# All edges but the fillers gathered by indirect DMA on one queue: the single-row loads of two other queues removed

## The chip, the cores and the metric

The kernel runs on one core of one Trainium2 chip. The metric is the device time in microseconds. The text calls the engines PE (TensorE), DVE (VectorE), ACT (ScalarE), POOL (GpSimd) and SP (SyncE).

## The reference

A graph layer over N = 50000 nodes with 128 features and E = 1650000 edges, sorted by target node. The edges hold one self edge per node. Each edge takes its source node's row through one of two weight matrices (by its type), the messages are summed per target, the node's own transform is added, then come ReLU, the residual and a norm without gain or offset.

```python
def _L0_gnn_ref(X, edge_index, edge_types, W_data, b_data, W_control, b_control, W_self, b_self):
    src, dst = (edge_index[0], edge_index[1])
    Xs = X[src]
    m_data = Xs @ W_data.T + b_data
    m_ctrl = Xs @ W_control.T + b_control
    msg = jnp.where((edge_types == 0)[:, None], m_data, m_ctrl)
    agg = jax.ops.segment_sum(msg, dst, num_segments=X.shape[0])
    out = agg + (X @ W_self.T + b_self)
    return jax.nn.relu(out)
...
x = _layernorm(x + _L0_gnn_ref(x, edge_index, edge_type_2, ...), axis=-1)
```

## The kernel before

The sum over edges is made before the weights: for each target node the source rows are summed per edge type, and only those sums are multiplied by the two weight matrices.

The sorted edge list is cut into 435 blocks. A middle block has 3800 edges: four steps (Q = 4) of seven chunks of 128 edges (R = 7, CH = 128) with 22 fillers each (F = 22), and at its end 128 edges (X) taken as single rows. The first and the last block are "plain": they have only chunks. For each chunk POOL issues one indirect DMA (L451) that gathers 128 rows of x, 64 KB, into a tile `y`. The pool of these tiles has 70 buffers, so that POOL can run ahead of its consumer. PE multiplies `y` by a one-hot matrix `oh` (L454) and adds up a step's seven chunks in a PSUM tile `acc`. The columns of `oh` are W target nodes, counted from the step's first target, for each of two edge types, so a step may not reach over more than W nodes. Two small matmuls (L457) add edge counts for the bias.

The fillers are edges that stand in the places of self edges: a self edge's source row is already in the block's window of x, so its chunk slot is given to a filler's source index, and the sum is put right with matrices made by `fill` and the `left_out_...` functions. `fill(b)` makes the index list `idxs[b]` that the gathers read, five blocks ahead (RAHEAD).

The 128 single rows of a block are loaded in `single_rows` (L434 and L439): SP and ACT each read 64 row offsets into registers and issue 64 DMAs of 512 bytes into a tile `yx`, a quarter of them in each step, two blocks ahead (AHEAD). The offsets come from a DVE op (`offsets`, L425). `yx` is a 29th chunk at the end of the block's last step (C1 = C + 1).

The instructions stand in program order on each engine (a manual schedule, written out in one loop over blocks). A block's four `add`s on DVE (L465) put `acc` into `sums`, a ring of three. Between blocks, ACT copies the overlapping part of the sums to the next ring entry (`take_over`, L470). On ACT's queue that copy stands behind the row DMAs of the block before. DVE then adds the left-out self edges (L363), PE makes the layer of the finished block (L475 to L478), DVE and ACT its norm (L483 to L497), and SP stores it (L498). SP also loads the windows of x (L387, L389) and, every ten blocks, the edge lists.

At the end the flag `bad` is computed. It is above 0 if a step reached over more than W nodes or had fewer than F self edges; then `general`, a slower program for any edge list, runs as well and overwrites the result.

Of the kernel before, what the change touches and what calls it, by code (L numbers as in the profile page):

```python
# [13 lines left out]
I32 = mybir.dt.int32  # L14
U8 = mybir.dt.uint8
AF = mybir.ActivationFunctionType
# [6 lines left out]
N = 50000  # L23
D = 128
ROW = 4 * D
E = 1650000
# [7 lines left out]
R = 7  # L34
W = 38
Q = 4
B = 128
C = R * Q
X = 128
C1 = C + 1  # L40
F = 22
BE = C * CH + Q * F + X
NBLK = 2 + (E - C * CH) // BE
# [5 lines left out]
GROUPS = -(-NBLK // GB)  # L49
GC = GB * C1  # L50
AHEAD = 2
# [27 lines left out]

def straight(ctx, tc, c, x, x_t, src_t, dst_t, etype_t, src_f, dst_f, etype_f, src_x, dst_first, first_p, out):  # L80


# [66 lines left out]

    one_g = {}  # L150

    def load_edges(g):
        t = eds.tile([1, GB * X], I32, name="one_g")
        nc.sync.dma_start(t, src_x[None, g * GB * X:(g + 1) * GB * X])
        one_g[g] = t
        loads[g] = {}
        for name, a in (("s", src_t), ("d", dst_t), ("t", etype_t)):
            t = eds.tile([P, GB, C1], I32, name=name, bufs=1)
            nc.sync.dma_start(t.rearrange("p b c -> p (b c)"), a[:, g * GC:(g + 1) * GC])
            loads[g][name] = t  # L160
        for name, a in (("sf", src_f), ("df", dst_f), ("tf", etype_f)):
            t = eds.tile([GS, F], I32, name=name, bufs=1)
            nc.sync.dma_start(t, a[g * GS:(g + 1) * GS, :])
            loads[g][name] = t
# [69 lines left out]
    def columns(g):  # L234

        a = loads.pop(g)
        first = begin[:, g * GB:(g + 1) * GB, :]
        steps = "p b (q r) -> p b q r"

        def first_of(rel, d):  # L240
            yield (rel[:, :, :C].rearrange(steps, r=R), d[:, :, :C].rearrange(steps, r=R),
                   first[:, :, :, None].to_broadcast([P, GB, Q, R]))
            yield rel[:, :, C:], d[:, :, C:], first[:, :, Q - 1:]

        def first_of_f(rel, d):
            yield rel, d, begin_p[:, g:g + 1].to_broadcast([GS, F])

        h = eds.tile([P, GB, Q, R + 1], BF16, name="h_loop", bufs=1)  # L250
        nc.vector.memset(h, 0.0)
        nc.vector.tensor_tensor(h[:, :, :, :R], a["s"][:, :, :C].rearrange(steps, r=R),
                                a["d"][:, :, :C].rearrange(steps, r=R), op=ALU.is_equal)
        rank = ps_r.tile([P, GB * Q, R + 1], F32, name="rank")
        hs_ = h.rearrange("p b q r -> p (b q) r")
        nc.tensor.matmul(rank, below, hs_, start=True, stop=False)
        for r in range(R):
            nc.tensor.matmul(rank[:, :, r + 1:], ones_b, hs_[:, :, r:r + 1].to_broadcast([P, GB * Q, R - r]),
                             start=False, stop=r == R - 1)

        col, rel = columns_of(a["d"], a["t"], first_of, "")
        check(a["d"], rel, [stats[:, 0, m, g:g + 1] for m in range(2)], "")
        col_f, rel_f = columns_of(a["df"], a["tf"], first_of_f, "_f")
        check(a["df"], rel_f, [stats[:GS, 1, m, g:g + 1] for m in range(2)], "_f")
        v = packed(a["s"], col, "")
        v_f = packed(a["sf"], col_f, "_f")

        cb = eds.tile([P, GB, C], F32, name="cb")
        nc.vector.tensor_scalar(cb, a["t"][:, :, :C], 0.0, float(P), op0=ALU.not_equal, op1=ALU.mult)
        nc.vector.tensor_tensor(cb, cb, a["d"][:, :, :C], op=ALU.add)  # L270
        nc.vector.tensor_tensor(cb, cb, base[:, g * GB:(g + 1) * GB, :].to_broadcast([P, GB, C]), op=ALU.subtract)


        rk = eds.tile([P, GB, C], F32, name="rk")
        nc.vector.scalar_tensor_tensor(rk.rearrange(steps, r=R), h[:, :, :, :R], -LOOP,
                                       rank.rearrange("p (b q) r -> p b q r", q=Q)[:, :, :, :R],
                                       op0=ALU.mult, op1=ALU.add)
        at = Q if g == 0 else 0
        n = (min((g + 1) * GB, NBLK - 1) - g * GB) * Q
        nc.vector.tensor_reduce(loops[:, g:g + 1], rank[:, at:n, R:], AX.XY, ALU.min)  # L280
        stay = eds.tile([P, GB, C], F32, name="stay")
        nc.vector.scalar_tensor_tensor(stay, rk, F - LOOP, v[:, :, :C], op0=ALU.is_ge, op1=ALU.mult)
        col_g[g], rk_g[g], stay_g[g], cb_g[g], vp_g[g] = col, rk, stay, cb, v_f
        if g == GROUPS - 1:
            idxs[NBLK - 1] = a["s"][:, NBLK - 1 - g * GB, :]
# [11 lines left out]
    def fill(b):  # L297
# [20 lines left out]
        nc.vector.tensor_single_scalar(idx, vi, 7, op=ALU.logical_shift_right)  # L318
        nc.vector.scalar_tensor_tensor(col_g[g][:, i, :C], idx, -float(P), vi, op0=ALU.mult, op1=ALU.add)
        idxs[b] = idx  # L320
# [44 lines left out]
    def chunks_of(b, q):  # L365

        n = C1 if not plain(b) else C if b == 0 else RCH if b < NBLK else 0
        return range(q * R, max(q * R, min((q + 1) * R if q < Q - 1 else C1, n)))

# [6 lines left out]
    bys, pcs, zs, pls = {}, {}, {}, {}  # L376
    ats = {}
    ohs, cnts, ys, accs, xws, xTs, pos, hs, mvs, sds = {}, {}, {}, {}, {}, {}, {}, {}, {}, {}

# [12 lines left out]
    def onehot(b):  # L392
        g, i = divmod(b, GB)
        n = C1 if not plain(b) else C if b == 0 else RCH
        oh = ohp.tile([P, C1, 2 * W], F32, name="oh")
        nc.vector.tensor_tensor(oh[:, :n, :], col_g[g][:, i, :n, None].to_broadcast([P, n, 2 * W]),  # L396
# [3 lines left out]
    def counts(b):  # L400

        cnt = ohp.tile([P, Q, 2 * W], BF16, name="cnt")
        with nc.allow_low_precision(reason="whole numbers up to R + 1"):
            whole = [q for q in range(Q) if len(chunks_of(b, q)) == R]
# [9 lines left out]

    SHARE = X // 2
    TURN = SHARE // Q
    RANGE = dict(min_val=0, max_val=(N - 1) * ROW, skip_runtime_bounds_check_because="where a node's row is")
    x_bytes = x.rearrange("n d -> (n d)").bitcast(U8)[None, :]

    def offsets(b):  # L420

        if not plain(b):
            g, i = divmod(b, GB)
            ats[b] = stp.tile([1, X], I32, name="at_x", bufs=AHEAD + 2)
            nc.vector.tensor_scalar(ats[b], one_g[g][:, i * X:(i + 1) * X], float(ROW), None, op0=ALU.mult)  # L425

    def single_rows(b, q):

        if q == 0:
            ys[b] = stp.tile([X, D], F32, name="yx", bufs=AHEAD + 2)  # L430
        both = []
        for j, (eng, dma) in enumerate(((SP, nc.sync), (ACT, nc.scalar))):
            at = j * SHARE + q * TURN
            _, rows = nc.values_load_multi_w_load_instructions(  # L434
                ats[b][0:1, at:at + TURN], engines=[eng], **RANGE)
            both.append([(dma, at + k, row) for k, row in enumerate(rows)])
        for pair in zip(*both):
            for dma, k, row in pair:
                dma.dma_start(ys[b][k:k + 1, :].bitcast(U8), x_bytes[:, bass.ds(row, ROW)])  # L439

    def products(b, q):
# [3 lines left out]
        for k in ks:  # L445
            if k == C:
                r, y = X, ys.pop(b)
            else:
                r = LAST if b == NBLK - 1 and k == RCH - 1 else P
                y = gat.tile([P, D], F32, name="y")  # L450
                nc.gpsimd.indirect_dma_start(  # L451
                    out=y[:r], out_offset=None, in_=x,
                    in_offset=bass.IndirectOffsetOnAxis(ap=idxs[b][:r, k:k + 1], axis=0))
            nc.tensor.matmul(acc[:, :2, :].rearrange("p t w -> p (t w)"), y[:r], ohs[b][:r, k, :],  # L454
                             start=k == ks[0], stop=k == ks[-1])
# [43 lines left out]

    for b in range(1, AHEAD + 1):  # L500
        offsets(b)
    columns(0)
# [6 lines left out]
    for b in range(1, RAHEAD):  # L509
# [3 lines left out]
        if b < AHEAD:  # L513
            onehot(b)
            counts(b)
            for q in range(Q):
                single_rows(b, q)
        if b == 1:
            clear_sums()
    for b in range(NBLK + 1):  # L520
# [16 lines left out]
        for q in range(Q):  # L537
# [24 lines left out]
            if q == 3:  # L562
                left_out_matrix(b + RAHEAD)
                offsets(b + AHEAD + 1)
            if not plain(b + AHEAD):
                single_rows(b + AHEAD, q)

# [251 lines left out]
def gnn_resnorm(  # L819
# [9 lines left out]
    etype_f: bass.AP,  # L829
    src_x: bass.AP,  # L830
    dst_first: bass.AP,
# [38 lines left out]
    with ExitStack() as own:  # L870
        straight(own, tc, c, x, x_t, src_t, dst_t, etype_t, src_f, dst_f, etype_f, src_x,
                 dst_first, first_p, out)
# [56 lines left out]
```

## Time and profile before

| | |
|---|---|
| Median of 10 runs | 15296.68 us (15284.49 to 15308.16) |
| The profiled execution | 15307.44 us |
| Its span on the page | 15305.4 us |
| POOL busy | 11521.9 us (75%) |
| PE busy | 7782.3 us (51%) |
| DVE busy | 6916.8 us (45%) |
| ACT busy | 353.7 us (2%) |
| Share of the 16 DMA engines, q0 (indirect) | 20.0% |
| Share of the 16 DMA engines, q1 and q10 | 3.4% and 0.4% |
| Mean granted TensorE clock | 1.000 |

Register, branch, semaphore and DMA-issuing instructions of a queue are not counted as busy, so ACT and SP can be occupied with issuing DMAs and still show almost no busy time. A group's row gives the instruction count, busy time and mean of one in ns, then the engine's idle time before these instructions and what ended most of it. A line of waits gives total us, times and the longest in us.

### The profile page before, as it was taken

To read this page: it belongs to the slowest core of one execution; us is meant where nothing else is said; L and a number is where in the kernel's file an instruction comes from. 1 tells how busy PE (TensorE), PEld (TensorE's weight loads), DVE (VectorE), ACT (ScalarE), POOL (GpSimd) and SP (SyncE) were. 2 spreads that over 40 slices of the span, in tenths; PEclk is the share of its full clock that TensorE was granted. 3 is DMA by queue.
4 is the path that set the end of the run, shared out by engine and by line. 5 is a ranking of instruction groups with operands and counts; after the bars stand their busy time and mean duration, and the time that the engine had idled before them with its cause. 6 is when DMAs were issued, how large, how long until landed. Compare 5 with 4: busy or idle time off the path is not lost.

```text
span 15305.4 us, 239078 instructions
## 1 busy us (share of the span) xinstructions
PE 7782.3 (51%) x34233; PEld 6914.0 (45%) x34234; DVE 6916.8 (45%) x12861; ACT 353.7 (2%) x875; POOL 11521.9 (75%) x12170
## 2 busy tenths in 40 slices
PE   4444444455555555666665544444444444444444
PEld 3444444444444444444444444444444444444444
DVE  5444444444444444444444444444444444444443
ACT  0000000000000000000000000000000000000000
POOL 7777777777777777777777777777777777777776
DMA  2222222222222222222222222222222222222222
GB/s 66 63 64 63 63 63 65 63 64 63 63 63 64 63 63 63 65 63 63 63 63 63 63 65 63 63 63 63 65 63 63 63 63 63 63 64 63 63 63 53
DMA packets 724494, 968.72 MB, mean 63 GB/s; under 512 B 282787, under 2 KB 522534, under 8 KB 722897
## 3 DMA queue, kind: packets, MB, share of 16 engines
q0 software_dynamic: 389120, 797.69, 20.0%
q1 hardware_dynamic: 277914, 141.12, 3.4%
q10 hardware_dynamic: 55862, 14.50, 0.4%
q14 instruction: 1315, 10.76, 0.2%
q8 instruction: 283, 4.64, 0.1%
HBM read 923.55 MB, written 28.66 MB: 62 GB/s over the span
## 4 chain that ended last, share of the span: by engine, by line
DMA 44%; ACTq 18%; issue 13%; SPq 11%; PE 8%; DVE 5%; ACT 1%; POOL 1%; DVEq 0%; POOLq 0%
DMA yx<-in_x 33%; ACTq L439 14%; SPq L439 9%; PE acc L454 6%; DMA y<-in_x,idx 6%; ACTq L434 3%; DMA out<-o 2%; DMA xT<-in_x_t 2%; DVE sums L363 1%; ACT sums L470 1%; POOL y L451 1%; DMA xw<-in_x 1%; SPq L381 1%; ACTq L468 1%; DMA vf_all<-vd 1%
## 5 line engine op out<-in xcount | busy, mean ns | idle before, releaser
L451 POOL DMA_INDIRECT y<-in_x,idx x12152 | 11512.8, 947 | 3711.9 <-issue 2069.0
L454 PE MATMUL acc<-oh,y 128*128 128x76 f32 x24320 | 6242.0, 429 | 1407.5 <-DMA y<-in_x,idx 1387.1
L454 PEld LDWEIGHTS acc<-oh,y 128*128 128x128 f32 x24320 | 5552.3, 327 | 1945.8 <-DMA y<-in_x,idx 1846.3
L363 DVE TENSOR_TENSOR sums<-pl,sums 128x384 f32<-128x384 f32 x433 | 241.6, 558 | 7506.5 <-ACT sums L470 7506.5
L349 PE MATMUL pl<-z,ones_b 88*128 88x256 bf16 x433 | 170.1, 393 | 3636.5 <-DVE sums L363 3553.3
L349 PEld LDWEIGHTS <-ones_b 88*128 88x128 bf16 x433 | 45.5, 105 | 3681.6 <-DVE sums L363 3681.6
L406 DVE TENSOR_REDUCE cnt<-oh 128x228 bf16<-128x1596 f32 (+2 forms) x435 | 1277.1, 2936 | 0.1
L333 PE MATMUL small<-ones_b,by 128*88 128x1 bf16 x433 | 99.0, 229 | 2246.6 <-DVE by L326 2153.7
L333 PEld LDWEIGHTS <-by 128*88 128x88 bf16 x433 | 64.2, 148 | 2289.5 <-DVE by L326 2289.1
L396 DVE TENSOR_TENSOR oh<-col,small 128x2204 f32<-128x2204 f32 (+2 forms) x435 | 1049.9, 2414 | 0.0
L457 PEld LDWEIGHTS <-to_row 128*128 128x128 bf16 x3476 | 633.5, 194 | 0.0
L465 DVE TENSOR_TENSOR sums<-acc,sums 128x114 f32 x1738 | 475.0, 273 | 298.4 <-PE acc L457 213.9
L326 DVE TENSOR_REDUCE by<-old 128x88 bf16<-128x616 f32 x433 | 577.9, 1335 | 14.8
L470 ACT COPY sums<-sums 128x384 f32 x434 | 222.2, 512 | 14154.5 <-DMA yx<-in_x 13437.5
L478 PE MATMUL po<-wmsgT,sums 128*128 128x128 f32 x1740 | 531.5, 461 | 0.0
L411 DVE TENSOR_REDUCE cnt<-oh 128x76 bf16<-128x608 f32 x434 | 503.9, 1161 | 0.0
L457 PE MATMUL acc<-cnt,to_row 128*128 128x38 bf16 x3476 | 473.5, 220 | 0.0
L478 PEld LDWEIGHTS po<-wmsgT,sums 128*128 128x128 f32 x1740 | 403.3, 322 | 97.5 <-issue 97.5
L307 DVE TENSOR_TENSOR m<-rk,small 128x616 f32<-128x616 f32 x433 | 344.5, 796 | 14.7
L310 DVE TENSOR_TENSOR new<-m,small 128x616 f32<-128x616 f32 x433 | 344.4, 795 | 14.8
L314 DVE TENSOR_REDUCE v_new<-new 128x28 f32<-128x616 f32 x433 | 344.2, 795 | 14.8
L476 PE MATMUL po<-bias,sums 3*128 3x128 f32 x870 | 344.5, 497 | 1.2 <-DVE sums L465 1.2
(116 smaller groups left out, 4064.8 us busy)
## 6 DMA issues: line engine op xcount, KB each, us to landing
yx<-in_x ACTq DMA_DIRECT2D x27712, 0.5 KB
yx<-in_x SPq DMA_DIRECT2D x27712, 0.5 KB
y<-in_x,idx POOLq DMA_INDIRECT x12152
xw<-in_x SPq DMA_DIRECT2D x435, 64.0 KB
xT<-in_x_t SPq DMA_DIRECT2D x435, 64.0 KB
out<-o SPq DMA_DIRECT2D x435, 64.0 KB
vf_all<-vd SPq DMA_DIRECT2D x44, 440.0 KB
s<-in_src_t SPq DMA_DIRECT2D x44, 145.0 KB
```

What stands on the lines that cost most here:

```text
L326: nc.vector.tensor_reduce(by, old.rearrange("p (q r) f -> p q f r", r=R), AX.X, ALU.add)
L363: nc.vector.tensor_tensor(part, pls.pop(b)[:, :, :B], part, op=ALU.add)
L396: nc.vector.tensor_tensor(oh[:, :n, :], col_g[g][:, i, :n, None].to_broadcast([P, n, 2 * W]), num_ps[:, None, :].to_broadcast([P, n, 2 * W ...
L406: nc.vector.tensor_reduce(cnt[:, :n, :], ohs[b][:, :n * R, :].rearrange("p (q r) w -> p q w r", r=R), AX.X, ALU.add)
L411: nc.vector.tensor_reduce(cnt[:, q, :], ohs[b][:, k[0]:k[-1] + 1, :].rearrange("p r w -> p w r"), AX.X, ALU.add)
L434: _, rows = nc.values_load_multi_w_load_instructions(ats[b][0:1, at:at + TURN], engines=[eng], **RANGE)
L439: dma.dma_start(ys[b][k:k + 1, :].bitcast(U8), x_bytes[:, bass.ds(row, ROW)])
L451: nc.gpsimd.indirect_dma_start(out=y[:r], out_offset=None, in_=x, in_offset=bass.IndirectOffsetOnAxis(ap=idxs[b][:r, k:k + 1], axis=0))
L454: nc.tensor.matmul(acc[:, :2, :].rearrange("p t w -> p (t w)"), y[:r], ohs[b][:r, k, :], start=k == ks[0], stop=k == ks[-1])
L457: nc.tensor.matmul(acc[:, 2, :], to_row[:, t, :], cnts[b][:, q, t * W:(t + 1) * W], start=t == 0, stop=t == 1)
L465: nc.vector.tensor_tensor(part, accs.pop((b, q)), part, op=ALU.add)
L478: nc.tensor.matmul(po, a[:, t, :B], c["wmsgT"][:, t * D:(t + 1) * D], start=False, stop=t == 1)
```

## The change

The single rows are taken out. A middle block now has 3672 edges, all in chunks but the fillers, so that there are 450 blocks and not 435; the last one has 11 chunks and not 8. The 29th chunk, `offsets`, `single_rows`, their tiles and their input array go. The one-hot's width W is 36 and not 38.

```diff
-W = 38
+W = 36
 Q = 4
 B = 128
 C = R * Q
-X = 128
-C1 = C + 1
 F = 22
-BE = C * CH + Q * F + X
+BE = C * CH + Q * F
...
-        n = C1 if not plain(b) else C if b == 0 else RCH if b < NBLK else 0
-        return range(q * R, max(q * R, min((q + 1) * R if q < Q - 1 else C1, n)))
+        n = RCH if b == NBLK - 1 else C if b < NBLK else 0
+        return range(q * R, max(q * R, min((q + 1) * R, n)))
...
-    def offsets(b):
-
-        if not plain(b):
-            g, i = divmod(b, GB)
-            ats[b] = stp.tile([1, X], I32, name="at_x", bufs=AHEAD + 2)
-            nc.vector.tensor_scalar(ats[b], one_g[g][:, i * X:(i + 1) * X], float(ROW), None, op0=ALU.mult)
-
-    def single_rows(b, q):
-
-        if q == 0:
-            ys[b] = stp.tile([X, D], F32, name="yx", bufs=AHEAD + 2)
-        both = []
-        for j, (eng, dma) in enumerate(((SP, nc.sync), (ACT, nc.scalar))):
-            at = j * SHARE + q * TURN
-            _, rows = nc.values_load_multi_w_load_instructions(
-                ats[b][0:1, at:at + TURN], engines=[eng], **RANGE)
-            both.append([(dma, at + k, row) for k, row in enumerate(rows)])
-        for pair in zip(*both):
-            for dma, k, row in pair:
-                dma.dma_start(ys[b][k:k + 1, :].bitcast(U8), x_bytes[:, bass.ds(row, ROW)])
-
     def products(b, q):
         g, i = divmod(b, GB)
         acc = ps.tile([P, 3, W], F32, name="acc")
         ks = chunks_of(b, q)
         for k in ks:
-            if k == C:
-                r, y = X, ys.pop(b)
-            else:
-                r = LAST if b == NBLK - 1 and k == RCH - 1 else P
-                y = gat.tile([P, D], F32, name="y")
-                nc.gpsimd.indirect_dma_start(
-                    out=y[:r], out_offset=None, in_=x,
-                    in_offset=bass.IndirectOffsetOnAxis(ap=idxs[b][:r, k:k + 1], axis=0))
+            r = LAST if b == NBLK - 1 and k == RCH - 1 else P
+            y = gat.tile([P, D], F32, name="y")
+            nc.gpsimd.indirect_dma_start(
+                out=y[:r], out_offset=None, in_=x,
+                in_offset=bass.IndirectOffsetOnAxis(ap=idxs[b][:r, k:k + 1], axis=0))
...
             if q == 3:
                 left_out_matrix(b + RAHEAD)
-                offsets(b + AHEAD + 1)
-            if not plain(b + AHEAD):
-                single_rows(b + AHEAD, q)
```

More of the change, by code (lines that the diff above doesn't have):

```diff
@@ L14 @@
 I32 = mybir.dt.int32
-U8 = mybir.dt.uint8
 AF = mybir.ActivationFunctionType
@@ L24 @@
 D = 128
-ROW = 4 * D
 E = 1650000
@@ L49 @@
 GROUPS = -(-NBLK // GB)
-GC = GB * C1
+GC = GB * C
 AHEAD = 2
@@ L77, in row_bcast, with straight @@
     return bass.AP(tensor=ap.tensor, offset=ap.offset, ap=[[0, n], *ap.ap])
-def straight(ctx, tc, c, x, x_t, src_t, dst_t, etype_t, src_f, dst_f, etype_f, src_x, dst_first, first_p, out):
+def straight(ctx, tc, c, x, x_t, src_t, dst_t, etype_t, src_f, dst_f, etype_f, dst_first, first_p, out):
     nc = tc.nc
@@ L148, in straight @@
     loops = keep.tile([P, GROUPS], F32, name="loops")
-    one_g = {}
     def load_edges(g):
-        t = eds.tile([1, GB * X], I32, name="one_g")
-        nc.sync.dma_start(t, src_x[None, g * GB * X:(g + 1) * GB * X])
-        one_g[g] = t
         loads[g] = {}
         for name, a in (("s", src_t), ("d", dst_t), ("t", etype_t)):
-            t = eds.tile([P, GB, C1], I32, name=name, bufs=1)
+            t = eds.tile([P, GB, C], I32, name=name, bufs=1)
             nc.sync.dma_start(t.rearrange("p b c -> p (b c)"), a[:, g * GC:(g + 1) * GC])
@@ L240, in first_of @@
         def first_of(rel, d):
-            yield (rel[:, :, :C].rearrange(steps, r=R), d[:, :, :C].rearrange(steps, r=R),
+            yield (rel.rearrange(steps, r=R), d.rearrange(steps, r=R),
                    first[:, :, :, None].to_broadcast([P, GB, Q, R]))
-            yield rel[:, :, C:], d[:, :, C:], first[:, :, Q - 1:]
         def first_of_f(rel, d):
@@ L251, in columns @@
         nc.vector.memset(h, 0.0)
-        nc.vector.tensor_tensor(h[:, :, :, :R], a["s"][:, :, :C].rearrange(steps, r=R),
-                                a["d"][:, :, :C].rearrange(steps, r=R), op=ALU.is_equal)
+        nc.vector.tensor_tensor(h[:, :, :, :R], a["s"].rearrange(steps, r=R),
+                                a["d"].rearrange(steps, r=R), op=ALU.is_equal)
         rank = ps_r.tile([P, GB * Q, R + 1], F32, name="rank")
@@ L268, in columns @@
         cb = eds.tile([P, GB, C], F32, name="cb")
-        nc.vector.tensor_scalar(cb, a["t"][:, :, :C], 0.0, float(P), op0=ALU.not_equal, op1=ALU.mult)
-        nc.vector.tensor_tensor(cb, cb, a["d"][:, :, :C], op=ALU.add)
+        nc.vector.tensor_scalar(cb, a["t"], 0.0, float(P), op0=ALU.not_equal, op1=ALU.mult)
+        nc.vector.tensor_tensor(cb, cb, a["d"], op=ALU.add)
         nc.vector.tensor_tensor(cb, cb, base[:, g * GB:(g + 1) * GB, :].to_broadcast([P, GB, C]), op=ALU.subtract)
@@ L281, in columns @@
         stay = eds.tile([P, GB, C], F32, name="stay")
-        nc.vector.scalar_tensor_tensor(stay, rk, F - LOOP, v[:, :, :C], op0=ALU.is_ge, op1=ALU.mult)
+        nc.vector.scalar_tensor_tensor(stay, rk, F - LOOP, v, op0=ALU.is_ge, op1=ALU.mult)
         col_g[g], rk_g[g], stay_g[g], cb_g[g], vp_g[g] = col, rk, stay, cb, v_f
@@ L318, in fill @@
         nc.vector.tensor_single_scalar(idx, vi, 7, op=ALU.logical_shift_right)
-        nc.vector.scalar_tensor_tensor(col_g[g][:, i, :C], idx, -float(P), vi, op0=ALU.mult, op1=ALU.add)
+        nc.vector.scalar_tensor_tensor(col_g[g][:, i, :], idx, -float(P), vi, op0=ALU.mult, op1=ALU.add)
         idxs[b] = idx
@@ L376, in straight @@
     bys, pcs, zs, pls = {}, {}, {}, {}
-    ats = {}
-    ohs, cnts, ys, accs, xws, xTs, pos, hs, mvs, sds = {}, {}, {}, {}, {}, {}, {}, {}, {}, {}
+    ohs, cnts, accs, xws, xTs, pos, hs, mvs, sds = {}, {}, {}, {}, {}, {}, {}, {}, {}
     def base_of(b):
@@ L393, in onehot @@
         g, i = divmod(b, GB)
-        n = C1 if not plain(b) else C if b == 0 else RCH
-        oh = ohp.tile([P, C1, 2 * W], F32, name="oh")
+        n = RCH if b == NBLK - 1 else C
+        oh = ohp.tile([P, C, 2 * W], F32, name="oh")
         nc.vector.tensor_tensor(oh[:, :n, :], col_g[g][:, i, :n, None].to_broadcast([P, n, 2 * W]),
@@ L402, in counts @@
         cnt = ohp.tile([P, Q, 2 * W], BF16, name="cnt")
-        with nc.allow_low_precision(reason="whole numbers up to R + 1"):
+        with nc.allow_low_precision(reason="whole numbers up to R"):
             whole = [q for q in range(Q) if len(chunks_of(b, q)) == R]
@@ L413, in counts @@
         cnts[b] = cnt
[L415 to L418, printed above, removed]
-    def offsets(b):
-        if not plain(b):
-            g, i = divmod(b, GB)
-            ats[b] = stp.tile([1, X], I32, name="at_x", bufs=AHEAD + 2)
-            nc.vector.tensor_scalar(ats[b], one_g[g][:, i * X:(i + 1) * X], float(ROW), None, op0=ALU.mult)
-    def single_rows(b, q):
-        if q == 0:
-            ys[b] = stp.tile([X, D], F32, name="yx", bufs=AHEAD + 2)
-        both = []
-        for j, (eng, dma) in enumerate(((SP, nc.sync), (ACT, nc.scalar))):
-            at = j * SHARE + q * TURN
-            _, rows = nc.values_load_multi_w_load_instructions(
-                ats[b][0:1, at:at + TURN], engines=[eng], **RANGE)
-            both.append([(dma, at + k, row) for k, row in enumerate(rows)])
-        for pair in zip(*both):
-            for dma, k, row in pair:
-                dma.dma_start(ys[b][k:k + 1, :].bitcast(U8), x_bytes[:, bass.ds(row, ROW)])
     def products(b, q):
@@ L498, in store @@
         nc.sync.dma_start(out[bass.ds(base_of(b), B), :], o)
-    for b in range(1, AHEAD + 1):
-        offsets(b)
     columns(0)
@@ L515, in straight @@
             counts(b)
-            for q in range(Q):
-                single_rows(b, q)
         if b == 1:
@@ L829, in gnn_resnorm @@
     etype_f: bass.AP,
-    src_x: bass.AP,
     dst_first: bass.AP,
@@ L870, in gnn_resnorm @@
     with ExitStack() as own:
-        straight(own, tc, c, x, x_t, src_t, dst_t, etype_t, src_f, dst_f, etype_f, src_x,
+        straight(own, tc, c, x, x_t, src_t, dst_t, etype_t, src_f, dst_f, etype_f,
                  dst_first, first_p, out)
@@ L894 @@
         rest = a[n:].reshape(TBL - 1, BE)
-        steps = rest[:, :Q * step].reshape(TBL - 1, Q, step)
-        cols = np.full((TBL, C1 * CH), pad, np.int32)
-        cols[0, :n] = a[:n]
-        cols[1:, :n] = steps[:, :, :R * CH].reshape(TBL - 1, n)
-        cols[1:, n:n + X] = rest[:, Q * step:]
-        cols[NBLK - 1, :n] = rest[NBLK - 2, :n]
-        cols[NBLK - 1, n:] = pad
+        steps = rest.reshape(TBL - 1, Q, step)
+        cols = np.full((TBL, C * CH), pad, np.int32)
+        cols[0] = a[:n]
+        cols[1:] = steps[:, :, :R * CH].reshape(TBL - 1, n)
+        cols[NBLK - 1] = rest[NBLK - 2, :n]
         fills = np.full((TBL, Q, F), pad, np.int32)
         fills[1:NBLK - 1] = steps[:NBLK - 2, :, R * CH:]
-        ones = np.full((TBL, X), pad, np.int32)
-        ones[1:] = rest[:, Q * step:]
         firsts = np.ascontiguousarray(cols[:, [q * R * CH for q in range(Q)]])
-        arrays[k + "_t"] = np.ascontiguousarray(cols.reshape(TBL * C1, CH).T)
+        arrays[k + "_t"] = np.ascontiguousarray(cols.reshape(TBL * C, CH).T)
         arrays[k + "_f"] = fills.reshape(TBL * Q, F)
-        if k == "src":
-            arrays["src_x"] = ones.reshape(-1)
         if k == "dst":
@@ L922 @@
         gnn_resnorm(tc, ap["x"], ap["x_t"], ap["src_t"], ap["dst_t"], ap["edge_type_2_t"], ap["src_f"], ap["dst_f"],
-                    ap["edge_type_2_f"], ap["src_x"], ap["dst_first"], ap["first_p"], ap["src"],
+                    ap["edge_type_2_f"], ap["dst_first"], ap["first_p"], ap["src"],
                     ap["dst"], ap["edge_type_2"],
```

## The prediction

> **What bounds the kernel now.** I read four views, in this order: the page's costliest groups, its chain that ended last, the waits of POOL and of ACT, and the gathers' line in two windows. The first two disagree, and the others settle it.
>
> Costliest groups and chain:
>
> ```profile
> L451 POOL DMA_INDIRECT y<-in_x,idx x12152 | 11512.8, 947 | 3711.9 <-issue 2069.0
> ...
> DMA yx<-in_x 33%; ACTq L439 14%; SPq L439 9%; PE acc L454 6%; DMA y<-in_x,idx 6%; ACTq L434 3%; DMA out<-o 2%; DMA xT<-in_x_t 2%; DVE sums L363 1%; ACT sums L470 1%; POOL y L451 1%; DMA xw<-in_x 1%; SPq L381 1%; ACTq L468 1%; DMA vf_all<-vd 1%
> ```
>
> The chain names the single rows (yx, issued at L439 by SP and ACT) for over half of the span and the gathers (y, issued by POOL at L451) for little. At face value the rows would be the bound. But POOL's own row adds up: 11512.8 busy + 3711.9 idle = 15224.7 us for 12152 gathers, 1.2529 us each, which fills a span of 15305.4 us. Whether POOL is a bound or only keeps pace hangs on that idle time. POOL's waits:
>
> ```profile
> POOL y L451 <- issue: 2071.5, 6783, 0.3
> POOL y L451 <- PE acc L454: 821.8, 2691, 0.3
> POOL y L451 <- DMA y<-in_x,idx: 496.2, 1624, 0.3
> ```
>
> Columns: total us, times, longest us. The longest wait is 0.3 us, and 2071.5 / 6783 is 0.305 us: the gap is the same whatever is named as its releaser, so it belongs to the issuing of a gather and is no wait. The gathers' line, first in a window before buffers are reused (the pool has 70, and 70 gathers take 88 us), then in the middle:
>
> ```profile
> L451 POOL DMA_INDIRECT y<-in_x,idx x17: 943/947/948, 39.7 to 59.7; - x17
> ...
> L451 POOL DMA_INDIRECT y<-in_x,idx x800: 941/947/1043, 6999.2 to 7999.4; - x160
> ```
>
> Shortest, median and longest in ns are alike in both, and the second gives 1000.2 us / 799 = 1.2518 us from start to start; there is no sign that POOL ever stands still for a buffer or an index. Last, are the gathers slower because rows are in flight? ACT issues its first row at 25.01 us, SP later still, and before that the timeline has
>
> ```profile
> 10.93 0.95 POOL L451 DMA_INDIRECT y<-in_x,idx  x1 [0.30 <-issue]
> 12.18 0.95 POOL L451 DMA_INDIRECT y<-in_x,idx  x1 [0.31 <-issue]
> 13.44 0.95 POOL L451 DMA_INDIRECT y<-in_x,idx  x1 [0.30 <-issue]
> 14.69 0.95 POOL L451 DMA_INDIRECT y<-in_x,idx  x1 [0.30 <-issue]
> ...
> 25.01 70.83 ACTq L439 DMA_DIRECT2D yx<-in_x  x128
> ```
>
> 3.76 us / 3 = 1.253 us with no row anywhere. So POOL issues gathers end to end at a pace that nothing else sets, and it is the bound. ACT is nearly one too: the longest entry of all waits is its own copy queued behind its row issues,
>
> ```profile
> ACT sums L470 <- DMA yx<-in_x: 13437.5, 410, 90.2
> ```
>
> and PE, which needs that copy's result, trails the gathers. Pairing each block's last gather with its last pair of y matmuls in the trace, PE trails by 2.6 us in the middle of the run and by up to 66 us towards the end. That lateness costs nothing while 70 buffers (88 us) cover it, and comes due at the end:
>
> ```profile
> 15241.30 0.99 POOL L451 DMA_INDIRECT y<-in_x,s  x1 [0.30 <-issue]
> ...
> 15282.76 0.55 PEld L454 LDWEIGHTS acc<-oh,y 120*128 120x128 f32 x2
> ```
>
> The last gather starts at 15241.3, its matmul 41.5 us later, and the span ends at 15305.4, 64.1 us after the last gather started.
>
> **The change, part by part.**
>
> Gathers added. Before, block 0 and 433 middle blocks have 28 chunks each and the last block 8: 434 x 28 + 8 = 12160 gathers (the page's 12152 and 8 more that read s). After, a middle block takes 28 x 128 + 88 = 3672 edges and not 3800, so there are 450 blocks, the last with 11 chunks: 449 x 28 + 11 = 12583. That is 423 more, on the engine that has no idle time: 423 x 1.2529 = 530.0 us, all on the path. The pace is bounded by 1.2500 below (the shortest step in the quiet stretch above) and 1.2533 above (1000.1 us / 798 in the window 1000 to 2000 us); over 12582 steps, and against the mean of 15233.1 / 12159 = 1.2528, that is -35 to +6 us. I take no change of pace, since the stretch without rows shows 1.253.
>
> A rule against this: the Trainium skill, "DMA: Bandwidth & Descriptors", section "Issuing engines are not separate DMA queues", says that starting DMAs from several engines saves only sequencer time, usually small beside the DMA. By it the return of 423 chunks to one issuer would cost little, and the time would be some 15260 us (the drain's gain below alone); the trace's 1.25 us of POOL per gather says that here the sequencer time is the whole cost.
>
> Rows removed. 433 blocks x 128 = 55424 row DMAs, 64 a block from ACT and 64 from SP, go, with their offset loads (L434) and the DVE op at_x (108.9 us in all). None of it lies on POOL. What it frees: ACT's copy L470 then waits for the previous block's last add (L465), which waits for that block's last gather. That copy still has a queue behind it, ACT's square root L489, and DVE and PE wait for both, but these take about a microsecond each in a block of 35 us. PE then trails by 2.6 us all through, as it does in the middle now. SP keeps windows, edge loads and stores; at 1 or 2 us of issuing per 35 us none of them is late.
>
> The drain. After the last gather starts: 2.6 us to its matmul, and from that matmul to the end as now, 15305.4 - 15282.8 = 22.6 us, together 25.2 against 64.1: a gain of 38.9 us. It is bounded by 0 (PE still late) and by about 41 (some of the 22.6 us is the norm of the block before, which can then be over earlier).
>
> Other engines. DVE: 6916.8 us over 435 blocks, 15.9 a block; the one-hot goes from 2204 to 2016 elements and the counts from 1596 + 608 to 2016, both smaller, so 450 blocks give about 6,900 us. PE: chunks 12160 + 433 = 12593 become 12583; the per-block work of 15 more blocks adds 15 x some 5 us to 7782.3. Both stay near half busy and cost nothing under POOL's 35.1 us a block; should POOL's cover fail, they would need some 18 us a block, so it cannot. Block 1's first index list is ready at 40.1 us and wanted at about 47 (gather 29 of the timeline); the prologue loses two at_x ops, so it is not later. Smaller loops of the group loads (280 instead of 290 columns) are hidden likewise.
>
> The sum, against the profiled execution: first gather at 8.2, plus 15233.1 to the last gather's start, plus 530.0, plus the drain of 25.2 = 15796.5 us span. The profiled run took 15307.44, 2.0 over its span: 15798.5. It was 10.8 over the median of the ten runs, 15296.68: **15788 us**, 3.2% slower. Against no change at all the measurement tells some 0.2%, 31 us.
>
> **The rivals.**
>
> *The gap is a wait after all (faster).* If the 0.30 us before each gather is held by something that trails because of the rows, PE's release of buffers above all, it goes, and 12582 x 0.947 + 8.2 + 25.2 gives about 11,950 us. The releaser names (PE, DMA y) and the chain's 33% for rows speak for it; the constant 0.3, and the same 0.30 before any buffer is reused and before any row is issued, speak against. It decides from 39 ns off each step: (530.0 - 38.9) / 12582. Chance 0.04.
>
> *The drain or the cover does not improve (still slower).* PE stays behind for another reason, or the index lists of the extra blocks hold POOL now and then: the time is 15788 + 39 = 15827 us. For it: ACT's copy, DVE and PE form a ring through every block. Against: its links are short, and in the middle of the run PE keeps up even with the rows. Chance 0.05.
>
> *The change does not do what it says.* Tile width W falls from 38 to 36. If a step's target nodes reach past it, or a step has under 22 self edges, the flag `bad` sends the kernel through general() as well: 400 x 35 = 14000 more gathers, 17,540 us, so over 33,300. From the reference's inputs the widest step reaches offset 35, the last that fits, and the fewest self edges are 24. Chance 0.01.
>
> **How the numbers follow.** The forecast has 0.90. Its range is the pace (-35 to +6) and the runs' own scatter (15284 to 15308, so about 12 either way); the second rival takes the top to 15827 + 8. That gives 15748 to 15835; left out are the first and third rivals and a little of the tails. Faster by over 0.2%: the first rival but for its end near 39 ns, 0.03. Within 0.2%: that end, 0.01. Slower: the forecast and the other two, 0.96.
>
> **What would show it.** Right: 12583 gathers in POOL's two rows (y from idx and y from s), 947 ns each with gaps of 0.3, the chain led by POOL's gathers or their landing; ACT's copy L470 waiting for DVE's add and no longer for yx; many short PE waits for y; the last matmul 2 to 3 us after the last gather and the span's end some 25 us after it. Wrong: a mean gather or gap shorter by tens of ns once rows are gone; gaps over 0.3 us on POOL, which would mean buffers or indices came late; a second pass of gathers after the flag.

## The result, and the profile after

The changed kernel takes **15788.4 us** (median of 8 runs, 15786.95 to 15789.86) beside 15298.5 us for the kernel before: a ratio of **1.0321**, 95% interval 1.0312 to 1.033. The profiled execution took 15788.39 us with a span of 15786.7 us. The numbers below marked "worked from the start times" come from the starts and ends of single gathers in a trace; a step is the time from one gather's start to the next one's.

The gathers' row on the page after (count, then busy us and mean ns of one, then the idle time before them):

```profile
L410 POOL DMA_INDIRECT y<-in_x,idx x12572 | 11909.8, 947 | 3831.8 <-issue 2521.3
```

The same page's chain that ended last, by line:

```profile
DMA y<-in_x,idx 43%; POOL y L410 8%; PE acc L413 8%; PE po L437 2%; PE po L435 2%; PE po L434 1%; DVE by L315 0%; PE acc L416 0%; DVE m L296 0%; PE pl L341 0%; DVE new L299 0%; DVE v_new L303 0%; PE pl L338 0%; DVE old L312 0%; POOLq L410 0%
```

With the 11 gathers that read s there are 12583 of them. The mean is 947 ns as before and the idle time is again 0.305 us a gather (3831.8 / 12572), though not one row DMA is left to wait for. The chain, which gave over half of the span to the rows, now runs through the gathers and their landing. POOL's waits, with total, times and longest:

```profile
POOL y L410 <- issue: 2524.1, 8282, 0.3
POOL y L410 <- DMA y<-in_x,idx: 600.3, 1970, 0.3
POOL y L410 <- PE acc L413: 492.9, 1617, 0.3
```

And ACT's:

```profile
ACT sums L429 <- DVE sums L424: 9214.1, 379, 83.6
```

No gap is over 0.3 us. ACT's copy (now L429) waits for DVE's last add (379 of 449 copies; the other 70 waits are put down to PE) and for no row any more. The end in the timeline:

```profile
15761.85 0.91 POOL L410 DMA_INDIRECT y<-in_x,s  x1 [0.30 <-issue]
...
15764.31 0.50 PEld L413 LDWEIGHTS acc<-oh,y 80*128 80x128 f32 x2 [0.64 <-DMA y<-in_x,s]
```

The matmul follows its gather by 2.5 us (41.5 before), and the drain is 15786.7 - 15761.85 = 24.9 us (64.1 before).

### The profile page after: what moved, and what is told of

It is laid out like the page before. It is cut to its first block, busy times and chain, and to the rows that moved or that the text cites. A ratio compares the mean times of both kernels' runs of the same rounds, so it can differ in the third digit from the quotient of the medians.

```text
span 15786.7 us, 123460 instructions
## 1 busy us (share of the span) xinstructions
PE 9734.5 (62%) x34521; PEld 7454.2 (47%) x34522; DVE 6948.2 (44%) x12350; ACT 365.8 (2%) x905; POOL 11921.7 (76%) x12593
## 4 chain that ended last, share of the span: by engine, by line
DMA 43%; issue 32%; PE 14%; POOL 8%; DVE 3%; POOLq 0%; DVEq 0%; SPq 0%; ACT 0%; ACTq 0%
DMA y<-in_x,idx 43%; POOL y L410 8%; PE acc L413 8%; PE po L437 2%; PE po L435 2%; PE po L434 1%; DVE by L315 0%; PE acc L416 0%; DVE m L296 0%; PE pl L341 0%; DVE new L299 0%; DVE v_new L303 0%; PE pl L338 0%; DVE old L312 0%; POOLq L410 0%
## 5 line engine op out<-in xcount | busy, mean ns | idle before, releaser
L410 POOL DMA_INDIRECT y<-in_x,idx x12572 | 11909.8, 947 | 3831.8 <-issue 2521.3
L413 PE MATMUL acc<-oh,y 128*128 128x72 f32 x25166 | 8328.4, 447 | 5732.9 <-DMA y<-in_x,idx 5694.5
L413 PEld LDWEIGHTS acc<-oh,y 128*128 128x128 f32 x25166 | 6236.3, 314 | 7757.8 <-DMA y<-in_x,idx 7088.0
L424 DVE TENSOR_TENSOR sums<-acc,sums 128x108 f32 x1798 | 487.1, 271 | 6271.2 <-PE acc L416 6205.3
L394 DVE TENSOR_REDUCE cnt<-oh 128x288 bf16<-128x2016 f32 x450 | 1672.5, 3717 | 0.1
L384 DVE TENSOR_TENSOR oh<-col,small 128x2016 f32<-128x2016 f32 x450 | 998.4, 2219 | 0.0
L429 ACT COPY sums<-sums 128x384 f32 x449 | 229.9, 512 | 10877.0 <-DVE sums L424 9214.1
L416 PE MATMUL acc<-cnt,to_row 128*128 128x36 bf16 x3596 | 481.0, 217 | 0.0
L312 DVE TENSOR_TENSOR old<-m,small 128x616 f32<-128x616 f32 x448 | 352.3, 786 | 0.0
L434 PE MATMUL po<-wselfT,xT 128*128 128x128 f32 x900 | 349.4, 492 | 0.0
L435 PEld LDWEIGHTS po<-bias,sums 3*128 3x128 f32 x900 | 223.9, 308 | 100.9 <-DVE sums L424 100.7
```

The costliest lines, as they stand in the source:

```text
L394: nc.vector.tensor_reduce(cnt[:, :n, :], ohs[b][:, :n * R, :].rearrange("p (q r) w -> p q w r", r=R), AX.X, ALU.add)
L410: nc.gpsimd.indirect_dma_start(out=y[:r], out_offset=None, in_=x, in_offset=bass.IndirectOffsetOnAxis(ap=idxs[b][:r, k:k + 1], axis=0))
L416: nc.tensor.matmul(acc[:, 2, :], to_row[:, t, :], cnts[b][:, q, t * W:(t + 1) * W], start=t == 0, stop=t == 1)
L424: nc.vector.tensor_tensor(part, accs.pop((b, q)), part, op=ALU.add)
L434: nc.tensor.matmul(po, xTs.pop(b), c["wselfT"], start=True, stop=False)
L435: nc.tensor.matmul(po, a[0:3, 2, :B], bias, start=False, stop=False)
```

## The experiments

Kernels that were sent together share the runs of the kernel before. Beside the experiments the kernel before took 15240 to 15244 us and not 15298 (22079 in one job, named below), so each is read by its own comparison. What I wanted to tell apart: is a gather's 1.25 us on POOL the price of the change (my theory), or the 15 more blocks and the narrower tiles, or a pace that the rows had held back?

**The rows taken away, nothing put in their place.** In the kernel before:

```diff
...
-                offsets(b + AHEAD + 1)
-            if not plain(b + AHEAD):
-                single_rows(b + AHEAD, q)
...
-        ks = chunks_of(b, q)
+        ks = [k for k in chunks_of(b, q) if k < C]
...
```

> The kernel before with its 435 blocks and 12160 gathers, but without the row DMAs, their offset loads and the DVE op that makes the offsets; the product of the 29th chunk is left out, so 55424 edges are missing from the sums. Theory (POOL's gathers are the bound, the rows are free to it): first gather at 8.1, 12159 steps of 1.252 us, a drain of 25 us, 1.7 around the span: 15258 us, 0.26% under before; if the step is the median one of the run after, 1.249, it is 15222. Rival 1 (the extra time of the change comes with the 15 extra blocks and the narrower tiles, not with gathers, and the rows cost nothing at all): as before, 15297. Rival 2 (rows were the bound, as the chain of waits has it): far below, under 14900.

15248.5 us beside 15240.4: ratio 1.0005 (0.9991 to 1.0019). Its gathers' row:

```profile
L451 POOL DMA_INDIRECT y<-in_x,idx x12152 | 11496.9, 946 | 3703.7 <-DMA y<-in_x,idx 2034.8
```

Without any row DMA a gather still takes 946 ns and its gap (3703.7 / 12152) 0.305 us. Within that interval, some -14 to +29 us, 55424 row DMAs were free to the kernel, though the chain put over half the span on them, and rival 2 falls. The 0.26% that the theory expected from an earlier end did not come; a later trace of the kernel before shows why (it has an early end too). Rival 1 expected no change as well, so the next run had to decide.

**One gather fewer in each middle block.** In the changed kernel:

```diff
-            y = gat.tile([P, D], F32, name="y")
-            nc.gpsimd.indirect_dma_start(
-                ...
+            if k != 1 or plain(b):
+                y = gat.tile([P, D], F32, name="y")
+                nc.gpsimd.indirect_dma_start(
+                    ...
```

> The changed kernel with one gather fewer in each of its 448 middle blocks: chunk 1 is multiplied from chunk 0's rows, so 57344 edges get the wrong source. Blocks, matmuls and DVE work are all as after. Theory (each gather costs POOL 1.252 us and nothing else counts): 15788 - 448 x 1.252 = 15227 us. Rival (the 450 blocks' work sets the time): near 15788.

15220.6 us, ratio 0.9986 (0.9972 to 1.0001).

```profile
L411 POOL DMA_INDIRECT y<-in_x,idx x12124 | 11482.4, 947 | 3694.7 <-DMA y<-in_x,idx 1845.7
```

450 blocks and all matmuls are there, and the loss is gone. The changed kernel itself stands at 1.0354 (below), so 448 gathers are worth 0.0368 x 15242 = 561 us, 1.252 us each; the two intervals leave some 32 us either way, 1.18 to 1.32 us a gather. The traces are closer: the last gather starts 559.8 us earlier than in the changed kernel's second trace, 1.250 us for each of the 448 (worked from the start times). That is the step of the trace, and it leaves nothing for blocks that these runs could show.

**Rows put back as idle load.** In the changed kernel, with `single_rows` as it was before but offsets from a fixed table:

```diff
...
+            if not plain(b + AHEAD):
+                single_rows(b + AHEAD, q)
+            if q == Q - 1 and b > AHEAD and b in ys:
+                u = stp.tile([1, 1], F32, name="used")
+                nc.vector.tensor_copy(u, ys.pop(b)[0:1, 0:1])
```

> The changed kernel, all computation kept, with row DMAs put back as idle load: SP and ACT each load 64 offsets a block (from a fixed table of 128 rows) and issue 64 DMAs of 512 bytes into a tile that only a 1 x 1 copy reads. Theory (rows cost POOL 3 ns a gather at most, and their main price is that ACT's copy and square root queue behind them, which makes PE late at the end): between 15788 + 0 and + 80, most likely 15836 (drain back from 25 to some 64 us, 12582 x 0.7 ns of pace). Rival (rows and gathers slow each other where both are issued): over 16200, 39 ns or more a gather.

15878.7 us, ratio 1.0418 (1.0403 to 1.0432): 0.0064 x 15242 = 98 us over the changed kernel, more than the 80 I allowed. The rival (over 16200) falls. POOL's waits and ACT's name the cause:

```profile
POOL y L434 <- PE acc L437: 782.2, 2373, 2.4
...
ACT sums L453 <- DMA yx<-in_x: 14400.7, 440, 35.8
```

And the timeline has the last gather at

```profile
15803.18 0.91 POOL L434 DMA_INDIRECT y<-in_x,s  x1 [0.30 <-issue]
```

Gaps of up to 2.4 us before a gather appear, which no earlier trace has: from 9.3 ms on PE is so late that all 70 buffers are taken and POOL stands. The start times show it: 71 gathers have a longer gap there, and such a gather typically starts 0.27 us after the end of the matmul that read its buffer, 70 gathers back. ACT's copy, which PE needs, stands behind the rows. The mean step is 1.2500 us between 1000 and 5000 us of the span and 1.2624 after 10000 (worked from the start times), and the drain is 15872.0 - 15803.2 = 68.8 us. So rows leave the gathers alone until the cover of 88 us is used up. Then PE, behind ACT's queue, holds POOL back.

**The same two kernels once more, on one chip, and the tile width alone.** The last run's edit is `W = 38` for `W = 36` in the changed kernel.

> The kernel before, unchanged, for its trace on this chip. Theory (the time is a tie of two paces, POOL's 28 x 1.25 us a block and ACT's row issues, and the second one differs a little from chip to chip): if the time is near 15297, the last matmul trails the last gather by 30 us or more and the drain is 50 to 70 us; if it is near 15240, as beside the last runs, PE trails by some 3 us at the end and the drain is 25 us; the gathers' step is 1.249 to 1.253 us in both. Rival (POOL's own pace differs between the chips): the drain is 60 us in both and the step is shorter by 3 to 5 ns where the kernel is faster.

> The changed kernel, unchanged, on this chip. Theory: it has no rows to pace, so it hardly differs between chips: 15765 to 15790 us, a drain of 25 us, and the loss against the kernel before is 490 us where that one has a late drain and some 530 us where it has not. Rival (the chips differ in POOL's pace): it moves with the kernel before, so that the ratio stays at 1.032.

> The changed kernel with the tile width W = 38 as before: the one-hot, the products and the adds are 5% wider, the 12583 gathers are the same. Theory (PE and DVE are hidden behind POOL): the time of the changed kernel on this chip, within 10 us. Rival (part of the loss or of a hidden gain comes from the narrower tiles): 1 to 2% more.

The kernel before: 15240.0 us in its profiled run. The changed kernel: 15782.5, ratio 1.0354 (1.0338 to 1.0369). With W = 38: 15782.8, ratio 1.0354 (1.0338 to 1.037), so the width is worth nothing that these runs show. The end of the kernel before in this trace:

```profile
15211.27 0.99 POOL L451 DMA_INDIRECT y<-in_x,s  x1 [0.30 <-issue]
...
15215.34 0.55 PEld L454 LDWEIGHTS acc<-oh,y 120*128 120x128 f32 x2
```

The last matmul trails by 4.1 us and the drain is 15238.0 - 15211.3 = 26.7 us, where the first trace had 41.5 and 64.1. In the last blocks PE is 25 us late and not 66 (paired block by block as in the prediction, whose "up to 66" is the level of the last blocks; near 14.8 ms single blocks have 29 and 70). So the drain does decide part of the difference between 15240 and 15298. My rival there was partly right too: the median step is 1.249 us here and 1.252 in the first trace, with the rows in flight in both. The gathers' line in the middle of this run (shortest, median and longest in ns):

```profile
L451 POOL DMA_INDIRECT y<-in_x,idx x799: 940/944/1231, 7000.3 to 7999.0; - x200
```

And in the changed kernel beside it:

```profile
L410 POOL DMA_INDIRECT y<-in_x,idx x800: 940/944/1172, 6999.8 to 7999.7; - x160
```

The 3 ns between 947 and 944 belong to the execution, not to the rows. The change costs 490 us against a kernel before with a late drain and 538 against one without. I had expected 490 and some 530. Between the two traces here the spans differ by 543.7 us: 423 gathers at 1.2504 us, the mean step of this kernel before, make 529, the drain gives back 2, and the remaining 17 us are steps that are 1.3 ns longer on average in the changed kernel (more on them below).

**ACT's copy on DVE.** In the kernel before, with rows; each block's store, which waits for ACT's square root, comes one block later too:

```diff
-        nc.scalar.copy(sums[b % RING][:, :, :B], sums[(b - 1) % RING][:, :, bass.ds(at, B)])
+        nc.vector.tensor_copy(sums[b % RING][:, :, :B], sums[(b - 1) % RING][:, :, bass.ds(at, B)])
...
-            if q == 1 and b > 0:
-                store(b - 1)
+            if q == 1 and b > 1:
+                store(b - 2)
...
```

> The kernel before, all rows kept, with the copy between blocks moved from ACT to DVE, and each block's store one block later so that ACT's square root may be late. Theory (PE trails by up to 66 us only because ACT's copy stands behind ACT's row issues; the lateness comes due in the drain): PE trails by 3 us, the drain is 25 us and the time 15258 us, 0.25% under before. Rival (something else makes PE late, or DVE has no room for 435 more copies of 0.5 us): 15297 or more.

15243.3 us beside 15240.4: ratio 1.0001 (0.9987 to 1.0015). As a gain this is inconclusive: beside it the kernel before took the time that goes with a short drain, so there was hardly one to cut. The mechanism does show: after the first three blocks (40 us late in block 0, as in the kernel before) PE trails by 2.5 us to the last block and never by more than 3.4 (worked from the start times). So it is what stands behind ACT's row issues that makes PE late, the copy or the square root that the store needs. The edit takes both out of the way; on the page of the kernel before, DVE waits 7506.5 us in all for the copy and 0.8 us for the square root, which speaks for the copy.

**A version that beats both.** If gathers are the price, fewer of them are the gain. To the last edit comes only:

```diff
-F = 22
+F = 24
```

> The kernel before with its rows kept, the copy between blocks on DVE and the store a block later, and F = 24 fillers a step and not 22: 434 blocks, the last of 11 chunks, 12135 gathers and not 12160. Theory (each gather is worth 1.25 us, and a late drain is cut to 25 us where there is one): 31 us under before on a chip with a drain of 25 us, some 70 us under it on one with 64. Rival (the wider fill on DVE, or ACT's and SP's row issues, set the pace instead): before or more.

15198.1 us beside 15244.3: ratio **0.997** (0.9959 to 0.9982), 46 us less. Its last gather:

```profile
15180.31 0.91 POOL L451 DMA_INDIRECT y<-in_x,s  x1 [0.30 <-issue]
```

It starts at 15180.31 and not at 15211.27, 31 us earlier for 25 gathers; 5 us more come from a drain of 21.6 us, and the rest is scatter. By the count in the prediction (no step with under 24 self edges) 24 is the most fillers that these inputs allow.

**Half the rows in each gather.** In the changed kernel, r = P // 2 in middle blocks.

> The changed kernel with each gather of the middle blocks cut to 64 rows of 128 (half of the edges are left out of the products); all 12583 gathers are issued. Theory (a gather's price is nearly all per DMA): from the run after, whose last gather of 80 rows took 910 ns beside 944 for 128, 0.71 ns a row, so 899 ns for 64: 12572 x 0.045 = 566 us less, some 15215 us. Rival (the price is per row): 472 ns and the same gap of 0.3 us, some 9850 us.

> The changed kernel with 64 rows in each gather of the middle blocks (half of the edges left out of the products), once more, for the same reason. In the first run the median step was 1.207 us for 64 rows beside 1.249 for 128. Theory (the price of a gather is nearly all per DMA): 8.2 + 12582 x 1.209 + 26 = 15246 us. Rival (per row): some 9850 us.

The first of these took 18016 us, in a job where the kernel before took 22079 and PE and DVE stood for up to some 20 us at many places in the traces; no total of that job is comparable, and what caused it is open. The second: **15247.1 us**, beside 15243.3 for the kernel before.

```profile
L410 POOL DMA_INDIRECT y<-in_x,idx x12572 | 11361.5, 904 | 3834.8 <-DMA y<-in_x,idx 2900.0
```

Half of the rows save 43 ns of 947. A gather of 64 rows keeps 97% of the price of one of 128 (1.209 us a step on average beside 1.252): the price is nearly all per DMA. The total is that of a single run; the step is read from its trace.

**A stretched gather.** The changed kernel's trace has gathers of over 1 us beside the op that makes z. It was written in another form:

```diff
-nc.vector.tensor_scalar(z..., node_no, at, None, op0=ALU.is_equal)
+nc.vector.tensor_tensor(z..., node_no, at.to_broadcast([Q * F, 2 * P]), op=ALU.is_equal)
```

> The changed kernel with the op that makes z (TENSOR_SCALAR, f32 to bf16, all in SBUF) written as a TENSOR_TENSOR with the scalar broadcast. In the changed kernel's trace 223 of 336 gathers that took over 40 ns more than the median lie beside this op and the add before it, 18.5 us of 41.9 us of such excess. Theory A (this op holds a port that the gathers' descriptors need): these long gathers go and the time falls by some 18 us, 0.1%. Theory B (the add, or any op with two inputs in SBUF, does it): long gathers stay or grow in number and the time is the same or up to 20 us more.

> The changed kernel with z made by a TENSOR_TENSOR, once more, since the kernel before took 22079 us beside its first run, so that nothing of 0.1% could be seen. Theory A (the TENSOR_SCALAR that made z holds up the gathers beside it): few gathers beside z and the add take over 40 ns more than the median, and the time is some 18 us under the changed kernel's 15782. Theory B (the add, or any op with two inputs in SBUF, does it): some 220 long gathers beside the two, 15782 to 15800 us.

The first ran in the same job of 22079 us (18048 us) and tells nothing. The second: 15807.2 us, ratio 1.0369 (1.0355 to 1.0383), some 23 us over the changed kernel by the ratios, whose intervals overlap. The op before and after:

```profile
L330 DVE TENSOR_SCALAR z<-node_no,at 88x256 bf16<-88x256 f32 x448 | 161.1, 360 | 16.0
...
L330 DVE TENSOR_TENSOR z<-node_no,at 88x256 bf16<-88x256 f32 x448 | 188.6, 421 | 15.6
```

356 gathers that start while z runs take over 40 ns more than the median, where the changed kernel has 223 and 116 in its two traces. All gathers that start in z together take 35.9 us more than the median, beside 11.3 in the changed kernel's second trace: that difference of 24.6 us is the difference of the two spans. Theory A falls. The add is cleared by the traces: of 61 gathers in the changed kernel and 19 in this one that start while it runs, none takes over 9 ns more than the median. So it is z that stretches them, in either form, and more with two inputs in SBUF.

The start times show how. A stretched gather's extra time and its start, counted from z's start, add up to the same sum: 0.223 us in the changed kernel (0.218 to 0.226 in nine of ten), 0.296 with TENSOR_TENSOR (0.292 to 0.299). Such a gather behaves as if it were held until a fixed moment of z. One that starts in the first 0.07 us of z, or after that moment, is not stretched. So the number of long gathers hangs on where in a step z falls, and differs between executions of one kernel.

## Why the prediction was right

- *The bound.* POOL's gathers end to end, with a gap that is no wait. It held: the gap is 0.305 us with rows, without them, and with half as many rows per gather. The rival that the gap is a wait fell with the first experiment.
- *423 gathers at 1.2529 us.* Measured at 1.252 each (1.18 to 1.32) by taking 448 away. The step after is 1.2521 us on average, 15753.8 / 12582; the forecast's mean was 1.2528.
- *No change of pace.* Right as a sum, by luck: two things that I did not see cancel. The median step fell from 1.252 to 1.249, below the 1.2500 that I had taken as the lower bound; that is 38 us over 12582 steps and belongs to the execution. And the mean lies above the median by 39 us in all, not by 10 (worked from the start times). Part of the second is the change's own doing, which I overlooked: 375 gathers start while z runs, where the kernel before has 28 and, in its second trace, 7, and they take 20 us more than the median. Leaving out the job of 22079 us, the traces without rows show 364 to 390 such gathers, the kernel before without rows too (364), and the traces with rows 7 to 40. Why z falls there without rows is open. Two kernels with 12135 gathers each show what all the longer steps come to, those beside other DVE ops included: the last gather starts at 15197.6 us in the changed kernel with one gather fewer a block and at 15180.3 in the version with F = 24, which keeps its rows.
- *The drain.* PE's lateness was read rightly and went with the rows. Forecast 25.2 us, measured 24.9. But the gain of 38.9 us is that of one kernel before with a late PE; against the second trace of it, it is 2 us.
- *Hidden work.* DVE 6,900 forecast, 6948.2 measured. PE was mis-sized: 7782 plus some 75 forecast, 9734.5 on the page. PE now takes each gather as it lands, two matmuls at a time, and two that stand alone cover 0.70 us of the timeline, where fourteen in a row cover 3.2 us, 0.46 a pair. It is not more work: the kernel before with its copy on DVE, where PE keeps up too, shows 9631.7 us for the matmuls of 7782.3. It cost nothing.
- *The last sum.* The span came out 9.8 us under the forecast 15796.5, and the median lay at the profiled run and not 10.8 under it. The hit to the microsecond is luck, these two cancelling; the steps are good to some 10 us.

## What to carry to other kernels

When the chain of waits and an engine's row disagree on the bound, look at that engine's gaps: a gap that is always the same, before any buffer is reused and whatever is named as its releaser, was the price of issuing here, and busy plus gap was the bound. Moving work from queues that run in parallel to the one that sets the time cost its full price there, so count the instructions on that queue first. A second queue close to the bound (here ACT's row issues: 1% over it in the run with rows put back, by the steps of 1.2624 and 1.2500 us) shows up as lateness that buffers cover; ask how much is left of the cover and what comes due at the end.

## What the runs showed of the hardware that was not expected

- An indirect DMA of 64 rows of 512 bytes costs POOL 1.209 us on average, one of 128 rows 1.252. From these two, 0.67 ns a row on a fixed 1.17 us is an estimate.
- A gather that starts while the op that makes z runs on DVE can be stretched: by 95 ns on average where z is a TENSOR_TENSOR, by 53 and 30 ns in two traces where it is a TENSOR_SCALAR, as if held until 0.296 or 0.223 us after z's start. One during which z starts and ends keeps its 944 ns. The Trainium skill, "SBUF — State Buffer", section "Who interferes with whom", says that a VectorE instruction with two inputs in SBUF contends with a GpSimd instruction that reads SBUF; the runs with TENSOR_TENSOR agree, and add that here only the start of a gather is exposed.
- The same kernel before took 15240 to 15244 us in three jobs, 15297 to 15298 beside the prediction and the result, and 22079 in one job. Between its two traces the spans differ by 67 us: 37 in the drain, from PE's lateness behind ACT's row issues, and 30 in the gathers' steps, 2.5 ns each. What makes either differ between executions is not settled.
